# Attention scores of two heads in one pair of PSUM banks, with mask, copy and maximum in one vector operation

## The chip, the cores and the metric

The kernel runs on one core of one Trainium2 chip. The metric is the device time of one execution in microseconds (us), lower is better; several executions are taken and the median is given. Five engines work side by side and meet only through semaphores: TensorE (PE) multiplies matrices, with a queue of its own for loading weights (PEld); VectorE (DVE), ScalarE (ACT) and GpSimd (POOL) work on whole tiles; SyncE (SP) issues most DMA transfers. Matmuls write to PSUM, which has eight banks of 128 partitions by 512 fp32 values.

## The reference

Eight images of 384 channels by 32 x 32 positions, thus 1024 tokens each, pass two layers. All numbers are fp32.

- Layer 0: an RMS norm over channels; a state-space branch (input projection, a causal convolution of four taps, SiLU, then a selective scan with 16 states per channel, once forwards and once backwards); a local branch (3 x 3 depthwise convolution and a sigmoid gate); their sum is added to the input.
- Layer 1, attention: a layer norm over channels, then six heads of size 64 over 1024 tokens, causal. For one head:

```
scores = q @ k^T
scores = where(column <= row, scores, -inf)
attn   = softmax(scores)            # over columns
out    = attn @ v
```

  The heads are joined, projected and added.
- Layer 1, feed-forward: for the first five images only (groups of eight divided by five give one image each): the weights are made binary around their group mean, `h = W1 x + b1` with 1536 rows is scaled by its largest absolute value and clipped, GELU, `W2 h + b2` is quantized in the same way, and the sum is added.

## The kernel before, in words

One image is 3 blocks of 128 channels by 1024 tokens, worked on in halves of 512 columns (`HB`), which is one PSUM bank. The eight banks are shared out by tag: one for `y` (the transposed scan output), two for `da` (the scan's decay factors), one for `av` (weighted values), and two each for `s` and `pt`. The function `bank` (line 101) gives one bank; asked without a tag it alternates between `s` and `pt`. Each bank is a tile of its own, which comes free when its last reader is done.

The work falls into stages that emit steps:

- `before_scan` (norm, projections, convolution, gates, the step size of the scan) takes its banks in turn from the tags that it is given: `s` and `pt` for the first four images, `pt`, `pt`, `av` for those that run later beside feed-forward. `binarize` prepares the feed-forward weights once, at the start; its group means are made in a matmul (line 228) into the bank `av`.
- The scan runs as 768 units of two states each: POOL multiplies `g` (line 588), ACT makes `da` (line 601), DVE scans two states one after the other (line 606), POOL multiplies again (line 612), and PE adds up the result by eight transposing matmuls into `y` (line 620). `g` has six buffers, so POOL can be ahead of PE by that much and no more.
- `attention` projects `op`, `qp`, `vp`, then works through three pairs of heads, two halves of the rows each. A score step (`scores`, lines 767 to 811) takes one block of 128 query rows and up to 512 key columns for the two heads of a pair. The heads lie in the upper and lower 64 rows of PE's array. Each gets its own bank of the tag `s`; the matmuls (line 786) are emitted for head 1 and then head 0, the second with a raised priority so that the two come out together where their banks allow it. In the block on the diagonal a bf16 matmul of an identity with the causal mask (line 797) adds the mask into the last 128 columns. Then, for each head, DVE takes the negated maximum of the bank (line 808) and ACT the exponential with the sum of its row (line 809):

```python
m = nm[:, i, e, kb : kb + 1]
nc.vector.tensor_reduce(m, s, AX.X, ALU.max, negate=True)
nc.scalar.activation(
    pr[:, e, : k1 - k0], s, AF.Exp, bias=m, accum_out=rs[:, i, e, kb : kb + 1]
)
```

  So a score bank is held until ACT has read it. In the step after, `turned` transposes the probabilities on PE (line 861) and ACT copies them (line 863), and `weigh` multiplies them with the values (line 874). There are 288 score steps in all.
- `feed_forward` makes `hp` (line 992), 12 blocks of two halves, and `yp` (line 1037), three blocks of two halves with 12 blocks to add up, each half in a bank of the tag `s`, so that one is filled while ACT empties the other (lines 1000 and 1045).

The order of the work is set in two steps. The program emits slots of the scan in between the steps of the other stages, by costs in microseconds written beside each step and by due times for each image's scan. Then a scheduler that works at build time orders the instructions of each engine by their priority (mostly the order of emission) and hands out the buffers. Each engine runs its own queue strictly in that order. The last image's attention is emitted after everything else.

Of the kernel before, what the change touches and what calls it, by code (L numbers as in the profile page):

```python
# [54 lines left out]
def kernel(  # L55
# [39 lines left out]

    BANKS = {"y": 1, "da": 2, "s": 2, "pt": 2, "av": 1}
    turn = [0]

    def bank(name, tag=None):
        if tag is None:  # L100
            turn[0] += 1
            tag = ("s", "pt")[turn[0] % 2]
        return ps.tile([P, HB], F32, name=name, tag=tag, bufs=BANKS[tag])

    def half(h):
# [51 lines left out]
    make_identity(nc, ident)  # L157
    identb = ctile("identb", [P, P], BF16)
    nc.vector.tensor_copy(identb, ident)
    cmask = mtile("cmask", P)  # L160
    make_causal_mask(nc, cmask, mask_val=MASKED)
    cmaskb = ctile("cmaskb", [P, P], BF16)
    nc.vector.tensor_copy(cmaskb, cmask)
    onesc = ctile("onesc", [P, P])
# [31 lines left out]
    def binarize(src, dst, nk, nout, per, name, emit):  # L196
# [15 lines left out]
        @emit  # L212
        def _():
            st["ones"] = small.tile([P, P], F32, name=f"ones_{name}", tag="bones", bufs=1)
            nc.vector.memset(st["ones"], 1.0 / (gs * nk * P))
            st["mps"] = bank(f"mps_{name}", "av")

        for k in starts:

            @emit  # L220
            def _(k=k, n=min(per, nk - k)):
                v = view(k, n)
                sums = small.tile([P, GROUPS], F32, name=f"sums_{name}_{k}", tag="bsums", bufs=1)
                for g in range(GROUPS):
                    nc.vector.tensor_reduce(
                        sums[:, g : g + 1], v[:, :, g * gs : (g + 1) * gs], AX.XY, ALU.add
                    )
                nc.tensor.matmul(
                    out=st["mps"][:, :GROUPS],
                    lhsT=st["ones"],  # L230
                    rhs=sums,
                    start=(k == 0),
                    stop=(k == starts[-1]),
                )

        @emit
        def _():
            st["mean"] = small.tile([P, GROUPS], F32, name=f"mean_{name}", tag="bmean", bufs=1)
            nc.vector.tensor_copy(st["mean"], st["mps"][:, :GROUPS])

# [17 lines left out]

    def mean_of(c_of, name):

        m = bank(name)
        for c in range(NC):
            nc.tensor.matmul(out=m, lhsT=onesc, rhs=c_of(c), start=(c == 0), stop=(c == NC - 1))
        return m
# [15 lines left out]
    def layernorm(src, name, emit):  # L280

        dst = src
        st = {}
        for h in range(NH):

            @emit.of(6.0)
            def _(h=h):
                mean = mean_of(lambda c: src()[:, c, half(h)], f"mean_{name}_{h}")
                for c in range(NC):
                    nc.vector.tensor_tensor(  # L290
                        dst()[:, c, half(h)], src()[:, c, half(h)], mean, ALU.subtract
                    )
                st[h] = squares(dst(), h, name)

        for h in range(NH):

            @emit.of(6.0)
            def _(h=h):
                var = mean_of(lambda c: st[h][c], f"var_{name}_{h}")
                rstd_of(var, 1)  # L300
                for c in range(NC):
                    nc.vector.tensor_tensor(  # L302
                        dst()[:, c, half(h)], dst()[:, c, half(h)], var, ALU.mult
                    )


    def before_scan(b, tags, emit, later=None, diags=None):
# [5 lines left out]
        def bank_of(name):  # L313
            return bank(name, next(turns))

# [7 lines left out]
        for h in range(NH):  # L323

            @emit
            def _(h=h):
                sqs = squares(st["xn"], h, f"n0_{b}")
                ms = mean_of(lambda c: sqs[c], f"ms_{b}_{h}")
                rstd_of(ms, 0)
# [344 lines left out]
    def attention(b, emit_ffn, emit):  # L674
# [12 lines left out]

        for h in range(NH):
            for m in range(NC):

                @emit
                def _(m=m, h=h):
                    op = bank(f"op_{b}_{m}_{h}")
                    for c in range(NC):
# [19 lines left out]
        for s in range(2):  # L714
            for m in range(NC):
                for h in range(NH):

                    @emit
                    def _(s=s, m=m, h=h):
                        if m == 0 and h == 0:  # L720
                            st["qk"[s]] = btile(f"{'qk'[s]}_{b}")
                        qp = bank(f"qp_{b}_{s}_{m}_{h}")
                        for c in range(NC):
# [9 lines left out]
        for j in range(NT):  # L733

            @emit
            def _(j=j):
                if j == 0:
                    st["v"] = btile(f"v_{b}").rearrange("p c l -> p (c l)").rearrange(
                        "p (j e) -> p j e", e=C
                    )  # L740
                vp = bank(f"vp_{b}_{j}")
                for c in range(NC):
# [24 lines left out]
        def probabilities(c, g, steps):  # L767
# [4 lines left out]
            def scores(i, qi, n, kb, k0, k1):  # L772
# [7 lines left out]
                nm, rs = st["nm", c, g], st["rs", c, g]  # L780
                ss = [bank(f"s_{b}_{c}_{qi}_{kb}_{e}", "s") for e in range(2)]

                order = (1, 0)
                for e in order:
                    with at_once(e == order[1]):
                        mm = nc.tensor.matmul(  # L786
                            out=ss[e][:, : k1 - k0],
                            lhsT=st["q"][rows_of(e), c, chunk(qi)],
                            rhs=st["k"][rows_of(e), c, k0:k1],
                            start=True,  # L790
                            stop=(k1 < n),
                        )
                    if e == order[1]:
                        pin(mm)
                if k1 == n:
                    for e in order:
                        mm = nc.tensor.matmul(  # L797
                            out=ss[e][:, k1 - k0 - P : k1 - k0],
                            lhsT=identb,
                            rhs=cmaskb,  # L800
                            start=False,
                            stop=True,
                        )
                        pin(mm)
                for e in range(2):
                    s = ss[e][:, : k1 - k0]
                    m = nm[:, i, e, kb : kb + 1]
                    nc.vector.tensor_reduce(m, s, AX.X, ALU.max, negate=True)  # L808
                    nc.scalar.activation(  # L809
                        pr[:, e, : k1 - k0], s, AF.Exp, bias=m, accum_out=rs[:, i, e, kb : kb + 1]  # L810
                    )
# [108 lines left out]
        for m in range(NC):  # L920
            for h in range(NH):

                @emit
                def _(m=m, h=h):
                    if h == 0:
# [4 lines left out]
                        st["to"] = to  # L930
                    op = bank(f"ap_{b}_{m}_{h}")
                    for c in range(NC):
# [21 lines left out]
    def quant_scale(mx, name):  # L954

        col = small.tile([P, 1], F32, name=f"col_{name}", tag="col")
        nc.vector.tensor_reduce(col, mx, AX.X, ALU.max)
        row = bank(f"row_{name}", "s")
        nc.tensor.transpose(row[:, :P], col.to_broadcast([P, P]), ident)
# [7 lines left out]
    def feed_forward(b, t, emit):  # L967
# [9 lines left out]
        for m in range(NF):  # L977
            for h in range(NH):

                @emit.of(3.1)  # L980
                def _(m=m, h=h):
                    if m % NC == 0 and h == 0:
                        st["h", m // NC] = btile(f"h{m // NC}_{b}")
                    if m % 2 == 0 and h == 0:
# [4 lines left out]
                        )  # L989
                    hp = bank(f"hp_{b}_{m}_{h}", "s")  # L990
                    for c in range(NC):
# [6 lines left out]
                        )  # L998
                    hm = st["h", m // NC][:, m % NC, :]
                    nc.scalar.activation(hm[:, half(h)], hp, AF.Identity, bias=b1t[:, m : m + 1])  # L1000
                    if h == NH - 1:
                        nc.vector.tensor_reduce(
                            st["mxh"][:, m : m + 1], hm, AX.X, ALU.max, apply_absolute_value=True
                        )
# [16 lines left out]
        for m in range(NC):  # L1021
            for h in range(NH):

                @emit.of(10.7)
                def _(m=m, h=h):
                    if m == 0 and h == 0:
                        st["y"] = btile(f"yf_{b}")
                    if h == 0:
                        for k in range(0, NF, 6):
# [4 lines left out]
                            st["w2", k // 6] = w  # L1034
                    yp = bank(f"yp_{b}_{m}_{h}", "s")
                    for k in range(NF):
# [6 lines left out]
                        )  # L1043
                    ym = st["y"][:, m, :]
                    nc.scalar.activation(
                        ym[:, half(h)], yp, AF.Identity, bias=vec[:, m, V_B2 : V_B2 + 1]
                    )
                    if h == NH - 1:
                        nc.vector.tensor_reduce(
                            st["mxy"][:, m : m + 1], ym, AX.X, ALU.max, apply_absolute_value=True  # L1050
# [6 lines left out]
        for m in range(NC):  # L1057

            @emit
            def _(m=m):  # L1060
                to = mtile(f"t3_{b}_{m}")
                load(to, spilled[b, "t2", m])
                for h in range(NH):
                    ym = bank(f"yq_{b}_{m}_{h}", "s")
                    nc.vector.tensor_scalar(
                        ym, st["y"][:, m, half(h)], st["s2"], QCLIP, ALU.mult, ALU.min
                    )
                    th = to[:, half(h)]
                    nc.vector.scalar_tensor_tensor(th, ym, -QCLIP, th, ALU.max, ALU.add)
                nc.sync.dma_start(out=out[b, chunk(m), :], in_=to)  # L1070
# [66 lines left out]
    begin = Steps()  # L1137
    before_scan(ORDER[0], ("s", "pt"), begin, beside)
    run(begin)
    beside += steps_of(before_scan, ORDER[1], ("s", "pt"), diags=diags)  # L1140
    beside += steps_of(binarize, w1, w1s, NC, FF, 2, "w1")
    beside += steps_of(binarize, w2, w2s, NF, C, 8, "w2")
    for b in ORDER[2 : 1 + ahead]:
        beside += steps_of(before_scan, b, ("s", "pt"), diags=diags)
    run(first, beside)
# [76 lines left out]
```

## Time and profile before

Three executions took 5177.72 to 5191.12 us, with a median of 5189.24. The profiled one took 5184.05 us and its span is 5182.2 us.

| engine | busy us | share of the span |
|---|---|---|
| PE | 4203.1 | 81% |
| PEld | 2254.6 | 44% |
| DVE | 3562.3 | 69% |
| ACT | 2701.1 | 52% |
| POOL | 3688.1 | 71% |

A page of the profile gives for each group of instructions the line, the engine, the operation, the tiles written and read, the shapes and the count; then the busy time and the mean of one in ns; then the time that the engine stood idle just ahead of such instructions, and what it waited for. An fp32 matmul counts as two instructions (two passes). Matmuls are pipelined, so the mean duration of one is longer than the time from one to the next. The table of waits sums idle time by who waited and for whom. Idle time of an engine that sets no pace costs nothing.

### The profile page before, as it was taken

The numbers are of one execution on the slowest core, as the hardware profiler recorded it, in microseconds if no ns is written. First come the engines' busy times: TensorE is split into PE (matmuls) and PEld (weight loads), VectorE is DVE, ScalarE is ACT, GpSimd is POOL, SyncE is SP. The second block draws the span as 40 slices with busy tenths as digits, with TensorE's granted clock in tenths as the row PEclk, the third lists the DMA queues.
The fourth block names the chain that finished last, engine by engine and source line by source line (L and its number), as shares of the span: only waits on it lengthen the run. The fifth ranks groups of instructions, "written<-read, shape, count | busy, mean of one in ns | idle before, by whom it ended". The sixth has DMA issues, their size and how long they took to land. (4 is left out here: it accounts for less than half of the span.)

```text
span 5182.2 us, 51037 instructions
## 1 busy us (share of the span) xinstructions
PE 4203.1 (81%) x16842; PEld 2254.6 (44%) x16842; DVE 3562.3 (69%) x4206; ACT 2701.1 (52%) x4891; POOL 3688.1 (71%) x1944
## 2 busy tenths in 40 slices
PE   3687787888878788888887888878889888888798
PEld 1243443444434444444543444434445444444444
DVE  6887887667886667876687856778666665565522
ACT  4565564555645556545556445564454454453334
POOL 0578687877679776787777788677878977787600
PEclk7788797889889899898998888988988889989888
DMA  6554545324463234543343533336333234224200
GB/s 228 197 184 152 200 167 190 111 80 156 152 216 114 88 103 146 198 143 112 109 153 121 201 126 103 118 125 221 122 103 126 88 106 166 87 70 150 82 33 25
DMA packets 365009, 696.38 MB, mean 134 GB/s; under 512 B 30104, under 2 KB 88904, under 8 KB 364744
## 3 DMA queue, kind: packets, MB, share of 16 engines
q1 hardware_dynamic: 355232, 676.97, 38.8%
q10 hardware_dynamic: 9512, 16.15, 0.9%
q8 instruction: 133, 2.18, 0.2%
q14 instruction: 132, 1.08, 0.1%
HBM read 527.33 MB, written 165.68 MB: 134 GB/s over the span
## 5 line engine op out<-in xcount | busy, mean ns | idle before, releaser
L588 POOL TENSOR_TENSOR g<-ud,bc 128x1024 f32<-128x1024 f32 x768 | 1836.3, 2391 | 737.0 <-PE y L620 586.5
L612 POOL TENSOR_TENSOR g<-g,bc 128x1024 f32<-128x1024 f32 x768 | 1818.8, 2368 | 229.8 <-DVE g L606 177.2
L601 ACT ACTIVATE da<-dl,amat 128x512 f32<-128x512 f32 x1536 | 1059.6, 692 | 1648.4 <-DVE g L606 1606.5
L606 DVE TENSOR_TENSOR_SCAN g<-da,carry,g 128x512 f32<-128x512 f32 x768 | 955.9, 1271 | 461.6 <-POOL g L588 430.2
L606 DVE TENSOR_TENSOR_SCAN g<-da,g 128x512 f32<-128x512 f32 x768 | 904.2, 1209 | 514.4 <-POOL g L588 496.9
L620 PE MATMUL y<-ident,g 128*128 128x128 f32 x6144 | 948.4, 301 | 272.7 <-POOL g L612 204.3
L620 PEld LDWEIGHTS y<-ident,g 128*128 128x128 f32 x6144 | 787.7, 156 | 663.0 <-POOL g L612 325.3
L786 PE MATMUL s<-k,q 64*128 64x512 f32 (+3 forms) x1152 | 443.6, 616 | 182.3 <-ACT pr L809 172.3
L808 DVE TENSOR_REDUCE nm<-s 128x1 f32<-128x512 f32 (+3 forms) x576 | 293.4, 543 | 231.0 <-PE s L797 154.9
L861 PE MATMUL pt<-ident,pr 128*128 128x128 f32 x1728 | 334.9, 315 | 80.0 <-ACT ptn L863 49.0
L809 ACT ACTIVATE pr<-s,nm 128x512 f32<-128x512 f32 (+3 forms) x576 | 327.8, 573 | 123.5 <-DVE nm L808 122.7
L992 PE MATMUL hp<-t,w 128*128 128x512 f32 x720 | 339.1, 616 | 25.8 <-DMA w<-w1s 15.1
L341 PE MATMUL in<-xn,win 128*128 128x512 f32 x576 | 295.2, 655 | 49.7 <-DVE xc L463 16.6
L1037 PE MATMUL yp<-h,w 128*128 128x512 f32 x720 | 327.5, 612 | 9.0 <-DMA w<-w2s 8.9
L861 PEld LDWEIGHTS pt<-ident,pr 128*128 128x128 f32 x1728 | 221.5, 159 | 238.7 <-ACT ptn L863 118.5
L863 ACT COPY ptn<-pt 128x512 f32<-128x512 f32 (+3 forms) x576 | 264.0, 480 | 101.8 <-PE pt L861 100.1
L874 PE MATMUL av<-ptn,v 128*64 128x512 f32 (+3 forms) x1152 | 287.9, 575 | 35.8 <-DVE o L888 21.0
L786 PEld LDWEIGHTS s<-k,q 64*128 64x128 f32 x1152 | 164.3, 212 | 323.6 <-ACT pr L809 254.8
L725 PE MATMUL qp<-t,wqk 128*128 128x512 f32 x576 | 263.0, 606 | 18.4 <-DVE t L302 13.0
L400 DVE SCALAR_TENSOR_TENSOR loc<-xn,vec,loc 128x496 f32<-128x496 f32 (+3 forms) x384 | 260.4, 721 | 23.6 <-ACT loc L389 22.2
L611 POOL COPY carry<-g 128x2 f32<-128x2 f32 x384 | 83.4, 217 | 248.0 <-DVE g L606 240.3
L1037 PEld LDWEIGHTS yp<-h,w 128*128 128x128 f32 x720 | 139.8, 198 | 176.3 <-issue 165.4
(157 smaller groups left out, 4817.3 us busy)
## 6 DMA issues: line engine op xcount, KB each, us to landing
bc<-rows SPq DMA_DIRECT2D x512, 512.0 KB, 4.1
dl<-sdl SPq DMA_DIRECT2D x160, 256.0 KB, 2.9
ud<-sud SPq DMA_DIRECT2D x160, 256.0 KB, 2.7
t<-st SPq DMA_DIRECT2D x63, 512.0 KB, 5.3
su<-u SPq DMA_DIRECT2D x48, 512.0 KB, 3.7
du<-su SPq DMA_DIRECT2D x96, 256.0 KB, 4.3
sdl<-du SPq DMA_DIRECT2D x96, 256.0 KB, 2.9
sud<-du SPq DMA_DIRECT2D x96, 256.0 KB, 2.7
```

What stands on the lines that cost most here:

```text
L341: nc.tensor.matmul(out=mp, lhsT=st["win", c][:, k, i, :], rhs=st["xn"][:, k, half(h)], start=(k == 0), stop=(k == NC - 1),)
L588: pin(nc.gpsimd.tensor_tensor(g, ud, sst["bc", 0, u.b, u.part, u.n], ALU.mult))
L601: nc.scalar.activation(da, sst["dl", u.b, u.c, u.part], AF.Exp, scale=amat[:, u.c, n : n + 1])
L606: nc.vector.tensor_tensor_scan(gi[:, ::step], da[:, ::step], gi[:, ::step], first, ALU.mult, ALU.add)
L612: pin(nc.gpsimd.tensor_tensor(g, g, sst["bc", 1, u.b, u.part, u.n], ALU.mult))
L620: nc.tensor.matmul(out=y[:, j, :], lhsT=g[:, i, chunk(j)], rhs=ident, is_transpose=True, start=(u.opens and i == 0 and j == 0), stop=(u.cl ...
L786: mm = nc.tensor.matmul(out=ss[e][:, : k1 - k0], lhsT=st["q"][rows_of(e), c, chunk(qi)], rhs=st["k"][rows_of(e), c, k0:k1], start=True, st ...
L808: nc.vector.tensor_reduce(m, s, AX.X, ALU.max, negate=True)
L809: nc.scalar.activation(pr[:, e, : k1 - k0], s, AF.Exp, bias=m, accum_out=rs[:, i, e, kb : kb + 1])
L861: nc.tensor.transpose(pt[:, chunk(i)], pr[:, e, chunk(j % QT)], ident)
L992: nc.tensor.matmul(out=hp, lhsT=st["w1"][:, c, chunk(m % 2)], rhs=st["xn"][:, c, half(h)], start=(c == 0), stop=(c == NC - 1),)
L1037: nc.tensor.matmul(out=yp, lhsT=st["w2", k // 6][:, k % 6, :], rhs=st["h", k // NC][:, k % NC, half(h)], start=(k == 0), stop=(k == NF - 1),)
```

## The change

The two banks of the tag `s` become one tile of two neighbouring banks, a pair. The scores of two heads fill one pair, always together. The causal mask is no longer added on PE: one vector operation reads a head's bank, adds the mask, multiplies by -1, writes the result to SBUF and takes the minimum, which is the negated maximum that the exponential needs as its bias. Blocks off the diagonal take a zero column of the mask, repeated. The exponential then works in place in SBUF, with a scale of -1. This operation, `tensor_tensor_reduce` with an output for the minimum, is built as two vector instructions, the second one writing the minimum.

The other stages that used `s` take pairs as well: `op`, `qp`, `vp`, `ap` and the layer norms' mean and variance alternate between a pair and two banks of `pt`; `hp`, `yp` and the quantization of the output use the pair as 1024 columns, emptied by one operation; `before_scan` of the first images rotates through `s` (half of a pair), `pt`, `av`, `pt`; the weights' group means move from `av` to a pair. The purpose is to take work from PE, to free the score banks earlier, and to empty banks in fewer operations.

The diff, cut to its core:

```diff
-    BANKS = {"y": 1, "da": 2, "s": 2, "pt": 2, "av": 1}
+    BANKS = {"y": 1, "da": 2, "s": 1, "pt": 2, "av": 1}
...
+    def pair(name):
+        return ps.tile([P, 2, HB], F32, name=name, tag="s", bufs=BANKS["s"])
+
+    def two_banks(name):
+        turn[0] += 1
+        if turn[0] % 2:
+            p = pair(name)
+            return [p[:, i, :] for i in range(2)]
+        return [bank(f"{name}_{i}") for i in range(2)]
...
+    cmask = ctile("cmask", [P, HB], BF16)
+    nc.vector.memset(cmask, 0.0)
+    masked = mtile("masked", P)
+    make_causal_mask(nc, masked, mask_val=MASKED)
+    nc.vector.tensor_copy(cmask[:, HB - P :], masked)
...
-            st["mps"] = bank(f"mps_{name}", "av")
+            st["mps"] = pair(f"mps_{name}")[:, 0, :]
...
-                        qp = bank(f"qp_{b}_{s}_{m}_{h}")
+                        if h == 0:
+                            st["qp"] = two_banks(f"qp_{b}_{s}_{m}")
+                        qp = st["qp"][h]
...
-                ss = [bank(f"s_{b}_{c}_{qi}_{kb}_{e}", "s") for e in range(2)]
-
-                order = (1, 0)
-                for e in order:
-                    with at_once(e == order[1]):
+                ss = pair(f"s_{b}_{c}_{qi}_{kb}")[:, :, : k1 - k0]
+                for e in range(2):
+                    with at_once(e == 1):
                         mm = nc.tensor.matmul(
-                            out=ss[e][:, : k1 - k0],
+                            out=ss[:, e, :],
                             lhsT=st["q"][rows_of(e), c, chunk(qi)],
                             rhs=st["k"][rows_of(e), c, k0:k1],
                             start=True,
-                            stop=(k1 < n),
-                        )
-                    if e == order[1]:
+                            stop=True,
+                        )
+                    if e == 1:
                         pin(mm)
-                if k1 == n:
-                    for e in order:
-                        mm = nc.tensor.matmul(
-                            out=ss[e][:, k1 - k0 - P : k1 - k0],
-                            lhsT=identb,
-                            rhs=cmaskb,
-                            start=False,
-                            stop=True,
-                        )
-                        pin(mm)
+
+                w = k1 - k0
+                mask = cmask[:, HB - w :] if k1 == n else cmask[:, :1].to_broadcast([P, w])
                 for e in range(2):
-                    s = ss[e][:, : k1 - k0]
-                    m = nm[:, i, e, kb : kb + 1]
-                    nc.vector.tensor_reduce(m, s, AX.X, ALU.max, negate=True)
+                    x, m = pr[:, e, :w], nm[:, i, e, kb : kb + 1]
+                    nc.vector.tensor_tensor_reduce(
+                        out=x,
+                        in0=ss[:, e, :],
+                        in1=mask,
+                        scale=-1.0,
+                        scalar=-MASKED,
+                        op0=ALU.add,
+                        op1=ALU.min,
+                        accum_out=m,
+                    )
                     nc.scalar.activation(
-                        pr[:, e, : k1 - k0], s, AF.Exp, bias=m, accum_out=rs[:, i, e, kb : kb + 1]
+                        x, x, AF.Exp, bias=m, scale=-1.0, accum_out=rs[:, i, e, kb : kb + 1]
                     )
...
-                    hp = bank(f"hp_{b}_{m}_{h}", "s")
+                    if h == 0:
+                        st["hp"] = pair(f"hp_{b}_{m}")
+                    hp = st["hp"][:, h, :]
...
-                    hm = st["h", m // NC][:, m % NC, :]
-                    nc.scalar.activation(hm[:, half(h)], hp, AF.Identity, bias=b1t[:, m : m + 1])
                     if h == NH - 1:
+                        hm = st["h", m // NC][:, m % NC, :]
+                        nc.scalar.activation(
+                            hm,
+                            st["hp"].rearrange("p h l -> p (h l)"),
+                            AF.Identity,
+                            bias=b1t[:, m : m + 1],
+                        )
...
-                    yp = bank(f"yp_{b}_{m}_{h}", "s")
+                        st["yp"] = pair(f"yp_{b}_{m}")
+                    yp = st["yp"][:, h, :]
...
-    before_scan(ORDER[0], ("s", "pt"), begin, beside)
+    before_scan(ORDER[0], ("s", "pt", "av", "pt"), begin, beside)
```

## The prediction

> **What bounds the kernel now.** I read the engines' totals first, then the windows by stage, then the table of waits, then the groups.
>
> ```profile
> PE 4203.1 (81%) x16842; PEld 2254.6 (44%) x16842; DVE 3562.3 (69%) x4206; ACT 2701.1 (52%) x4891; POOL 3688.1 (71%) x1944
> ```
>
> No engine is full, but TensorE (PE) is the fullest. The windows say where (columns: window, its length, then busy us and instruction count of PE, PEld, DVE, ACT, POOL, then clock and DMA): one of attention beside scans, one of the stage before the scans beside feed-forward, and the end, where the last image's attention runs without scans.
>
> ```profile
> 3770.00:3900.00 130.00, 108.34 (x573) 62.11 (x573) 76.01 (x98) 69.66 (x165) 99.23 (x63) 0.83 0.29 96
> 2860.00:2990.00 130.00, 102.70 (x307) 52.35 (x306) 107.05 (x122) 57.25 (x93) 94.08 (x56) 0.84 0.55 189
> 4923.00:5182.00 259.00, 237.10 (x912) 110.15 (x912) 64.93 (x129) 97.24 (x258) 0.00 (x0) 0.87 0.08 29
> ```
>
> Attention loads PE (83%, at the end 92%) and leaves VectorE (DVE) 42% free. The other stage loads DVE (82%). The waits (engine and line, releaser: us in total, times, longest):
>
> ```profile
> ACT da L601 <- DVE g L606: 1606.5, 1104, 11.1
> POOL g L588 <- PE y L620: 586.5, 211, 11.3
> PEld s L786 <- ACT pr L809: 254.8, 273, 6.3
> PE s L786 <- ACT pr L809: 172.3, 141, 6.0
> ```
>
> The second row is the key one: GpSimd (POOL), which feeds the scan, stands 587 us because PE has not yet transposed the scan's output and so not freed a `g` buffer. PE works through one queue, in which transposes stand between attention's matmuls; what delays a score matmul delays the scan. The last row is such a delay: the score matmul finds its PSUM bank still held by the exp of the step before. In the attention window above, POOL makes 21 pairs of multiplications in 130 us, 6.2 us each, where two multiplications of 2.36 us take 4.7: POOL can follow a faster PE. So I treat PE time in attention as time of the kernel.
>
> The groups I price from (busy us, mean ns | idle before):
>
> ```profile
> L786 PE MATMUL s<-k,q 64*128 64x512 f32 (+3 forms) x1152 | 443.6, 616 | 182.3 <-ACT pr L809 172.3 <-DVE v L750 4.9 <-ACT v L750 4.2
> L797 PE MATMUL s<-cmaskb,identb 128*128 128x128 bf16 x384 | 61.9, 250 | 0.0
> L808 DVE TENSOR_REDUCE nm<-s 128x1 f32<-128x512 f32 (+3 forms) x576 | 293.4, 543 | 231.0 <-PE s L797 154.9 <-PE s L786 75.3
> L809 ACT ACTIVATE pr<-s,nm 128x512 f32<-128x512 f32 (+3 forms) x576 | 327.8, 573 | 123.5 <-DVE nm L808 122.7
> L809 ACT ACTIVATION_READ_ACCUMULATOR pr<-s,nm 128x1 f32 x576 | 113.3, 197 | 0.0
> L290 DVE TENSOR_TENSOR t<-t,mean_na 128x512 f32<-128x512 f32 x48 | 30.1, 676 | 12.8 <-PE mean_na L263 7.9 <-DMA st<-t 3.0 <-PE y L620 1.8
> L703 DVE SCALAR_TENSOR_TENSOR t<-op,rssm,t 128x512 f32<-128x512 f32 x48 | 34.4, 734 | 21.2 <-PE op L695 21.1
> L1000 ACT ACTIVATE h<-hp,b1t 128x512 f32<-128x512 f32 x120 | 80.3, 675 | 38.6 <-PE hp L992 38.4
> L434 ACT ACTIVATE u<-u 128x1024 f32<-128x1024 f32 x48 | 50.2, 1056 | 0.6
> ```
>
> [...]
>
> **The change part by part.**
>
> *Masks leave PE.* 384 bf16 matmuls go, 61.9 us of PE. Their weight loads stand idle another 97 us on the load queue, mostly beside other matmuls. Between 45 and 90; I take 62.
>
> *The two heads' score matmuls stay together.* They lie on different 64-row halves of the array. In the last attention four 512-wide passes of such a pair take 1.13 us, where twelve full-height passes of L992 take 5.15, 0.43 each: the heads run at the same time, and apart they would need four times 0.43, 1.72. In the built order of before, other work stands between the heads in 77 of the 288 score steps, since each head waits for its own bank; with one pair tile, the order of after has 288 of 288 together. A split costs 0.6 us at 512 and, at the mean width of 384, 0.45: 77 x 0.45 = 35 us. Low 20, high 50.
>
> *The bank comes free earlier.* Before, from the scores' end: two maxima and the last exp with its accumulator read, 0.54 + 0.54 + 0.57 + 0.20 = 1.85 us at the mean width, and that exp queues behind `da` exponentials that wait for scans (the 1606 us row). Now the DVE operation writes negated masked scores to SBUF, and exp works there: the pair is free after two DVE operations and their reads. An operation at 384 is 676 - 133 = 543 ns by L290 [...] or 734 - 133 = 601 by L703: I take 0.57. The read lies between 0.06 (the smallest memset of the trace, 59 ns) and 0.20 (ScalarE's): I take 0.13. Together 2 x 0.70 = 1.4 us, 0.45 less, and one queue fewer. The head that used to be free first now waits for both, a loss inside the same wait. Of the 172 us on PE I let 95 go; between 40 and 150.
>
> *DVE pays.* 576 x (0.57 + 0.13 - 0.51) = 109 us, with 0.51 = 293.4/576; between 60 and 160. DVE goes from 69% to 71%, and in the attention window from 76 to about 83 of 130. What queues behind are scans, and POOL behind those (it waits 177 us for scans today). I let a quarter through: 27 us; between 0 and 60.
>
> *Exp from SBUF.* Same width, another source, ScalarE at 54% in the attention window: nothing, hidden behind PE. `ptn` copies wait no longer than before.
>
> *Feed-forward on one pair.* `hp` and `yp` had two banks in turn; now 75 pairs share one tile, evicted by one activation of 1024 elements (1.06 by L434, against 2 x 0.675: ScalarE saves 22 us, hidden). The new wait: the next pair's first matmul stands behind that activation, and behind it in PE's queue stand the scan's transposes. In the built order some 2 us of other PE work lies between one `hp` pair and the next (1.2 to 4.3, of transposes and input projections), against 1.06 plus the hand-over. Mostly hidden; a late ScalarE gives perhaps 0.3 us each: 22 us, between 0 and 100 (75 x 1.3).
>
> *Other users of the pair* (`op`, `qp`, `vp`, `ap`, layer norm) keep four banks in rotation, only freed two at a time: 10 us. In the first stage four banks rotate as before, but the weights' mean takes the pair where it had a bank unused at that time, so the binarization moves from the first 100 vector instructions to the 350th. DVE is at 65% in the first 130 us and 87% in the next two windows, so work moved out of the idle start costs: 15 us, between 0 and 40. Halved quantization (`yq`) and dropped memsets: some 5 us of DVE, hidden.
>
> Sum: 62 + 35 + 95 - 27 - 22 - 10 - 15 = 118 us of gain. 5189 - 118 = 5071; I say 5070.
>
> **The rivals.**
>
> *Slower: DVE becomes the bound.* If the new operation runs at half rate, it takes about 1.0 us at the mean width, the pair's chain grows to 2.3 us, longer than before, and DVE gets 576 x (1.0 + 0.13 - 0.51) = 357 us. With half of that on the path (scans sit in that queue), and the waits not shrinking but growing by 40, against 97 from masks and pairing: 5189 + 178 + 40 - 97 + 47 = 5357; with full rate but every feed-forward wait exposed (100), DVE's 60 and the start's 40: 5189 - 62 - 35 - 40 + 100 + 60 + 40 + 10 = 5262. For it: DVE is nearly full outside attention. Against: [...]attention is where DVE has room.
>
> *No change: the waits move.* PE's score wait turns from ACT into DVE at the same length, as scans of 1.2 us stand in between, and the additions eat the masks: 5189 - 62 - 35 + 27 + 22 + 10 + 15 = 5166, with somewhat more wait 5185. For it: POOL, DVE and PE feed each other in a ring, and PE still waits 204 us for POOL. Against: the last attention has no scans, waits 15 us at L786 and spends 7.9 us on masks; it must gain.
>
> *Much faster.* All score waits but a few vanish (150), masks are worth 90, pairing 50, no new stall: 5189 - 290 + 20 = about 4920.
>
> **How the numbers follow.** Forecast, within about 60 us: 0.56. Much faster: 0.12. Waits move: 0.16, half of it still a little faster than 0.3%. Slower: 0.16. So faster 0.56 + 0.12 + 0.07 = 0.75, same 0.08, slower 0.17. The range runs from 4960 to 5215: above it is most of the slower case, below it half of the much faster one.
>
> **What would show it.** Right: the score matmuls wait for the new vector line, under 110 us on PE; no mask line; busy time of the score matmuls falls below 420 us with fewer split pairs; POOL waits for PE under 500 us; the last attention, from its first `op` matmul, takes 235 to 245 us instead of 259; the new vector operation takes 0.68 to 0.74 at 512 and its read 0.06 to 0.20. Wrong: the operation over 0.9 us at 512; scans that wait behind it so that POOL's wait for scans passes 300 us; `hp` matmuls that wait over 50 us for their activation; a first `y` transpose or a last scan that comes later than today. An instruction order that the planner changes by chance could also shift the stages by more than the terms I priced.

## The result, and the profile after

The changed kernel takes 5243.63 us (median of four executions, 5241.31 to 5251.63), the kernel before 5187.74 in the same comparison. The ratio is 1.0114, with a 95% interval of 1.0096 to 1.0131: it is slower by about 56 us, where a gain of 118 was forecast.

The totals of the changed kernel's page (busy us, share, instructions):

```profile
PE 4073.2 (78%) x16458; PEld 2177.5 (41%) x16458; DVE 3606.6 (69%) x4755; ACT 2701.9 (51%) x4812; POOL 3703.7 (71%) x1944
```

PE has 130 us less to do than before (4203.1) and the span is 67.6 us longer (5249.8 against 5182.2). So PE stands idle 198 us more. The granted clock of the whole run does not explain that: it is 0.872 to 0.876 in the four executions, and 0.870 to 0.877 in those of the kernel before that were taken beside the experiments. The waits of the changed kernel that answer to those shown of before, with the bank waits of the projections and of feed-forward added:

```profile
ACT da L612 <- DVE g L617: 1642.5, 1110, 10.7
POOL g L599 <- PE y L631: 724.8, 216, 16.0
PEld s L801 <- DVE nm L815: 254.8, 138, 6.2
PE s L801 <- DVE nm L815: 206.9, 112, 6.0
PE hp L1012 <- ACT h L1021: 50.7, 21, 8.4
PE op L708 <- DVE t L716: 31.9, 14, 6.2
PE vp L760 <- ACT v L767: 15.9, 11, 2.1
PE ap L951 <- DVE t L959: 14.4, 7, 3.7
PE qp L740 <- DVE k L747: 14.4, 7, 2.1
```

POOL waits 138 us longer for PE's transposes (586.5 before): the ring of POOL, scan and PE has become slower. The last five rows are new or longer. In the kernel before, PE waited 3.2 us at `op` for the reader of an earlier `op`, and `vp` and `ap` had no idle time at all. The groups of the changed kernel (busy, mean ns of one | idle before):

```profile
L801 PE MATMUL s<-k,q 64*128 64x512 f32 (+3 forms) x1152 | 310.0, 620 | 215.6 <-DVE nm L815 206.9 <-ACT v L767 6.3 <-DVE v L767 2.0
L815 DVE CUSTOM_DVE_ANT_0 pr<-s,cmask 128x512 f32<-128x512 f32 (+3 forms) x576 | 293.4, 546 | 148.5 <-PE s L801 115.1 <-PE pt L877 33.0
L815 DVE DVE_READ_ACCUMULATOR2_ANT nm<- 128x1 f32 x576 | 47.5, 82 | 0.0
L1021 ACT ACTIVATE h<-hp,b1t 128x1024 f32<-128x1024 f32 x60 | 66.2, 1103 | 42.0 <-PE hp L1012 41.8
```

At 512 columns the new operation, with mask, scaling and output, takes as long as the plain maximum of before:

```profile
L808 DVE TENSOR_REDUCE nm<-s 128x1 f32<-128x512 f32 x288 | 185.9, 676 | 102.7 <-PE s L786 75.3 <-PE s L797 27.2
L815 DVE CUSTOM_DVE_ANT_0 pr<-s,cmask 128x512 f32<-128x512 f32 x288 | 184.8, 679 | 37.6 <-PE s L801 37.4
```

The first row of L815 is the new vector operation; its accumulator read, 82 ns, is a row of its own. The mask matmuls are gone. The score matmuls are busy for 310 us instead of 444, but wait longer.

The stages tell where the time went. Going by when the same scan starts in both traces, the changed kernel lags 27 us at the 97th scan, 53 at the 577th, 79 at the 1057th and 103 at the 1489th of 1536; then the last attention takes back 38. The end, from the last scan on (columns as in the windows of before; first the kernel before, then the changed one):

```profile
4899.00:5182.00 283.00, 251.32 (x985) 119.14 (x983) 77.02 (x150) 99.10 (x261) 5.49 (x3) 0.87 0.10 37
```

```profile
5005.00:5250.00 245.00, 213.10 (x936) 100.94 (x934) 77.66 (x217) 99.42 (x260) 5.40 (x3) 0.95 0.11 43
```

There the score stage, from its first to its last vector operation, falls from 146 to 104 us. So the change gains where no scans run; beside the scans something eats more than it brings. The 38 us need not all be the banks' doing, however: the granted clock (third number from the end) is 0.95 in this stretch against 0.87. As an estimate from these shares, 283 x 0.13 = 37 us of full clock were withheld before and 245 x 0.05 = 12 now, so up to 25 of the 38 us may be clock. Whether the shorter waits raised the clock is not shown.

### The profile page after: what moved, and what is told of

It is laid out like the page before. It is cut to its first block, busy times and chain, and to the rows that moved or that the text cites. A ratio compares the mean times of both kernels' runs of the same rounds, so it can differ in the third digit from the quotient of the medians.

```text
span 5249.8 us, 50688 instructions
## 1 busy us (share of the span) xinstructions
PE 4073.2 (78%) x16458; PEld 2177.5 (41%) x16458; DVE 3606.6 (69%) x4755; ACT 2701.9 (51%) x4812; POOL 3703.7 (71%) x1944
## 5 line engine op out<-in xcount | busy, mean ns | idle before, releaser
L599 POOL TENSOR_TENSOR g<-ud,bc 128x1024 f32<-128x1024 f32 x768 | 1842.5, 2399 | 868.1 <-PE y L631 724.8
L623 POOL TENSOR_TENSOR g<-g,bc 128x1024 f32<-128x1024 f32 x768 | 1826.7, 2379 | 262.4 <-DVE g L617 173.3
L801 PE MATMUL s<-k,q 64*128 64x512 f32 (+3 forms) x1152 | 310.0, 620 | 215.6 <-DVE nm L815 206.9
L877 PE MATMUL pt<-ident,pr 128*128 128x128 f32 x1728 | 323.4, 308 | 113.1 <-ACT ptn L879 74.5
L815 DVE CUSTOM_DVE_ANT_0 pr<-s,cmask 128x512 f32<-128x512 f32 (+3 forms) x576 | 293.4, 546 | 148.5 <-PE s L801 115.1
L825 ACT ACTIVATE pr<-pr,nm 128x512 f32<-128x512 f32 (+3 forms) x576 | 347.9, 606 | 77.4 <-DVE nm L815 76.4
L1012 PE MATMUL hp<-t,w 128*128 128x512 f32 x720 | 344.2, 624 | 51.8 <-ACT h L1021 50.7
L1063 PE MATMUL yp<-h,w 128*128 128x512 f32 x720 | 324.6, 608 | 14.5 <-DMA w<-w2s 10.2
L877 PEld LDWEIGHTS pt<-ident,pr 128*128 128x128 f32 x1728 | 208.2, 153 | 307.4 <-ACT ptn L879 151.8
L740 PE MATMUL qp<-t,wqk 128*128 128x512 f32 x576 | 285.6, 646 | 43.0 <-DVE t L312 23.8
L890 PE MATMUL av<-ptn,v 128*64 128x512 f32 (+3 forms) x1152 | 275.1, 562 | 21.4 <-DVE o L904 12.5
L1012 PEld LDWEIGHTS hp<-t,w 128*128 128x128 f32 x720 | 136.7, 198 | 218.8 <-issue 146.2
L801 PEld LDWEIGHTS s<-k,q 64*128 64x128 f32 x1152 | 99.3, 211 | 306.2 <-DVE nm L815 254.8
```

What stands on the lines that cost most here:

```text
L599: pin(nc.gpsimd.tensor_tensor(g, ud, sst["bc", 0, u.b, u.part, u.n], ALU.mult))
L623: pin(nc.gpsimd.tensor_tensor(g, g, sst["bc", 1, u.b, u.part, u.n], ALU.mult))
L740: nc.tensor.matmul(out=qp, lhsT=st["wqk"][:, c, o : o + P], rhs=st["xn"][:, c, half(h)], start=(c == 0), stop=(c == NC - 1),)
L801: mm = nc.tensor.matmul(out=ss[:, e, :], lhsT=st["q"][rows_of(e), c, chunk(qi)], rhs=st["k"][rows_of(e), c, k0:k1], start=True, stop=True,)
L825: nc.scalar.activation(x, x, AF.Exp, bias=m, scale=-1.0, accum_out=rs[:, i, e, kb : kb + 1])
L877: nc.tensor.transpose(pt[:, chunk(i)], pr[:, e, chunk(j % QT)], ident)
```

## Experiments

All results are given as the ratio to the kernel before in the same comparison. Its median was 5185.7 to 5190.8 us in these comparisons, so a difference of a few us between two runs means nothing.

Two theories stood at the start: the hand-over of banks in pairs costs (P), or the vector operation costs, as banks now wait in VectorE's queue (D).

**The operation alone.** The kernel before, with separate score banks, and only the vector operation taken over. To make room in SBUF for the wider mask, the group means use the common matrix of ones, as in the changed kernel.

```diff
-                    nc.vector.tensor_reduce(m, s, AX.X, ALU.max, negate=True)
...
+                    nc.vector.tensor_tensor_reduce(
+                        out=x,
+                        in0=ss[e][:, :w],
+                        in1=mask,
+                        scale=-1.0,
+                        scalar=-MASKED,
+                        op0=ALU.add,
+                        op1=ALU.min,
+                        accum_out=m,
+                    )
```

> The kernel before with the new vector operation alone: each head keeps its own score bank, op, qp, vp, ap, hp, yp and the layer norms keep their single banks. If the loss comes from handing banks over in pairs (theory P), the operation alone gains: 5060 to 5130 us, and the waits of PE at op, qp, vp, ap and hp stay at the sum of before, 65 us. If the operation itself is the cost (theory D: the banks now wait in VectorE's queue behind scans, and scans behind the operation), it is no faster than before: 5180 to 5260 us.

Measured: 5047.58 us, ratio 0.9725 (0.9709 to 0.9741). The operation alone gains some 141 us, and theory D falls. Its score group and its operation:

```profile
L785 PE MATMUL s<-k,q 64*128 64x512 f32 (+3 forms) x1152 | 405.4, 609 | 124.2 <-DVE nm L798 113.3 <-DVE v L749 4.9 <-ACT v L749 4.2
L798 DVE CUSTOM_DVE_ANT_0 pr<-s,cmask 128x512 f32<-128x512 f32 (+3 forms) x576 | 301.2, 546 | 212.0 <-PE s L785 185.3 <-PE pt L860 26.0
```

Busy and idle time of the score matmuls come to 405.4 + 124.2 = 530 us, against 310.0 + 215.6 = 526 with the pair, and in the last attention the score stage takes 98 us against 104 (the granted clock of the whole profiled run is 0.881, against 0.872). So at the scores themselves the pair brings almost nothing that the operation doesn't bring with separate banks.

**The pairs alone.** The changed kernel with the old mask matmuls, the old reduction and the exponential from PSUM.

> The changed kernel with masks on PE, maximum by the old reduction and exponential from PSUM: only the pairs are left. Theory P: slower than before by the added bank waits, 121 us at op, qp, vp, ap and hp, and by more score waits, since the pair needs both exponentials: 5270 to 5350 us. Theory D: about as before, 5180 to 5210 us.

Measured: 5861.52 us, ratio 1.1297 (1.128 to 1.1314), far beyond what theory P expected. A pair is now held until both exponentials are done. The idle time of PE that ends with an exponential goes from 172 us, all at the scores, to 314: 141.9 at the scores and 171.6 at the transposes of the probabilities. The built order shows a second cause. In all 288 score steps the maximum of the second head carries a wait for ScalarE's exponential of the first head, though that reads the other bank of the pair; in the kernel before, none of the 288 does. So VectorE stands still, with scans behind in its queue, and POOL's wait for PE more than doubles (586.5 before):

```profile
DVE nm L825 <- ACT pr L826: 126.2, 143, 1.9
POOL g L600 <- PE y L632: 1253.1, 128, 129.1
```

No run shows how the loss divides between the two. With the new operation VectorE alone reads the pair, and in the changed kernel none of its second heads carries a wait. So the two parts of the change depend on each other. The operation is worth 141 us with separate banks and 618 with pairs (5861.5 to 5243.6). The pairs cost 196 us with it (5047.6 to 5243.6) and about 673 without.

**Single banks for the projections.** The changed kernel, but `op`, `qp`, `vp`, `ap`, mean and variance take banks one by one.

```diff
-    def two_banks(name):
+    def single(name):
         turn[0] += 1
-        if turn[0] % 2:
-            p = pair(name)
-            return [p[:, i, :] for i in range(2)]
-        return [bank(f"{name}_{i}") for i in range(2)]
+        tag = ("s", "pt", "av", "pt")[turn[0] % 4]
+        return pair(name)[:, 0, :] if tag == "s" else bank(name, tag)
...
-                        if h == 0:
-                            st["qp"] = two_banks(f"qp_{b}_{s}_{m}")
-                        qp = st["qp"][h]
+                        qp = single(f"qp_{b}_{s}_{m}_{h}")
```

> The changed kernel, but op, qp, vp, ap and the layer norms rotate through four banks that come free one by one (half of the pair, pt, av, pt). Theory P: PE's waits at op, qp, vp and ap fall from 134 us to about 40, and the time by 60 to 95 us, to 5150 to 5185. Theory D: within 15 us of the changed kernel, 5230 to 5260.

Measured: 5117.85 us, ratio 0.9864 (0.9849 to 0.9878): 126 us less than the changed kernel, and more than theory P expected. PE's idle time at `op`, `qp`, `ap` and `vp` is 35 us instead of 134. First the changed kernel, then this one, where `ap` and `vp` have none:

```profile
L708 PE MATMUL op<-gy,wout 128*128 128x512 f32 x288 | 155.6, 694 | 54.6 <-DVE t L716 31.9 <-DVE du L538 13.5 <-DMA gy<-sgy 7.4
L740 PE MATMUL qp<-t,wqk 128*128 128x512 f32 x576 | 285.6, 646 | 43.0 <-DVE t L312 23.8 <-DVE k L747 14.4 <-ACT q L747 4.0
L951 PE MATMUL ap<-o,wproj 128*128 128x512 f32 x288 | 137.1, 624 | 14.4 <-DVE t L959 14.4
L760 PE MATMUL vp<-wv,t 128*128 128x384 f32 x384 | 135.6, 499 | 22.1 <-ACT v L767 15.9 <-DVE v L767 6.2
```

```profile
L700 PE MATMUL op<-gy,wout 128*128 128x512 f32 x288 | 147.1, 661 | 15.4 <-DVE du L532 6.2 <-DVE t L1080 4.8 <-DVE t L708 3.5
L730 PE MATMUL qp<-t,wqk 128*128 128x512 f32 x576 | 264.2, 609 | 20.0 <-DVE t L306 12.2 <-issue 5.6 <-DVE q L737 2.0
POOL g L593 <- PE y L625: 600.1, 201, 12.5
```

More was gained than these 99 us, and POOL's wait for PE, the last row, falls by 125 us, from 724.8: a late PE holds up POOL too. This is the largest single loss of the change.

**Emptied by halves.** The changed kernel, `hp` and `yp` emptied by two activations of 512.

```diff
+                    hm = st["h", m // NC][:, m % NC, :]
+                    nc.scalar.activation(hm[:, half(h)], hp, AF.Identity, bias=b1t[:, m : m + 1])
                     if h == NH - 1:
-                        hm = st["h", m // NC][:, m % NC, :]
-                        nc.scalar.activation(
-                            hm,
-                            st["hp"].rearrange("p h l -> p (h l)"),
-                            AF.Identity,
-                            bias=b1t[:, m : m + 1],
-                        )
```

> The changed kernel, but each half of hp and yp is emptied by its own 512-wide activation, as before; the pair stays one tile. Theory P, if the length of the last eviction (1.10 us against 0.67) makes the hp wait: PE's wait at hp falls from 52 us to about 30, time 5215 to 5235. If the wait is ScalarE's queue, or the missing second buffer as such, no change: 5235 to 5260. Theory D: no change.

Measured: 5318.91 us, ratio 1.0253 (1.0238 to 1.0268): slower by 75 us than the changed kernel, which no theory expected. The idle time at feed-forward rises from 51.8 us at `hp` and 14.5 at `yp` to:

```profile
L1012 PE MATMUL hp<-t,w 128*128 128x512 f32 x720 | 358.7, 636 | 68.4 <-ACT h L1020 68.0
L1058 PE MATMUL yp<-h,w 128*128 128x512 f32 x720 | 347.6, 642 | 39.7 <-ACT yf L1066 27.3 <-DMA w<-w2s 10.4 <-DVE h L1039 1.9
```

The built programs show why. In this kernel the first matmul of the second half carries a wait for ScalarE's reading of the first half in 59 of 60 `hp` tiles and 15 of 15 `yp`; in the changed kernel in none. Where a reader of the first half stands between the two halves, the build makes the second half's matmuls wait for it, though they write another bank: it guards the tile as a whole. The same holds for the projections of the changed kernel, in 62 of their 64 pair tiles. A piece of PE's built order (x2 stands for two matmuls alike):

```
Matmult qp_7_1_0 128x512 [waits Activation]
Matmult qp_7_1_0 128x512 x2
Matmult qp_7_1_1_0 128x512 [waits Activation]
Matmult qp_7_1_0 128x512 [waits Activation]
Matmult qp_7_1_0 128x512 x2
```

The tile `qp_7_1_0` is a pair: its first half waits for the slot, and its fourth matmul, the first of the second half, waits again. One matmul of the next block, into the single bank `qp_7_1_1_0`, is put in between. In the trace of the changed kernel one sees the wait at the end of the last image's projections, with no scan to disturb (time, duration, engine; PE, then ACT; in brackets the idle time before):

```profile
5107.61 2.20 PE L760 MATMUL vp<-wv,t 128*128 128x384 f32 x6 [0.57 <-ACT v L767]
```

```profile
5107.08 0.48 ACT L767 COPY v<-vp 128x384 f32<-128x384 f32 x1 [1.46 <-PE vp L760]
```

The copy ends at 5107.56, and the matmuls of the second half start 0.05 us later, after 0.57 us of idle PE.

**Both halves before the emptying.** This gave a third theory, L (lock), against W, that only the shorter rotation of banks costs. The changed kernel keeps its pairs, but in the projections both halves are multiplied before either is read:

```diff
-                        nc.any.tensor_copy(st["qk"[s]][:, m, half(h)], qp)
+                        if h < NH - 1:
+                            return
+                        for i in range(NH):
+                            nc.any.tensor_copy(st["qk"[s]][:, m, half(i)], st["qp"][i])
```

> The changed kernel with its pairs, but in op, qp, vp, ap and the layer norms both halves are emptied after the second half's matmuls, not the first half in between. Theory L (lock: in one tile the second half's matmuls are made to wait for the reader of the first half): PE's waits at op, qp, vp and ap fall from 134 us to under 60, the time to 5110 to 5165 us. Theory W (window: a pair comes free only as a whole, so the rotation of banks is shorter): no gain, as the first half is emptied even later: 5240 to 5290 us.

Measured: 5160.46 us, ratio 0.9937 (0.9922 to 0.9951). With the same pairs in the same banks, 83 us of the 126 come back, and the kernel is now faster than before. In the built order none of the 64 pair tiles has a wait for a reader in the middle; idle time at the four projections is 59 us (31.9 + 27.2 + 0 + 0). Theory L holds for two thirds. The remaining 43 us fit theory W, that a pair comes free as a whole, but no run isolates that; the run with single banks also takes the bank `av` into the rotation.

**Feed-forward on single banks.** The run with single projections, and `hp` and `yp` in single banks too, each emptied by itself.

> The run with single banks for the projections, and hp and yp in single banks as well (half of the pair, pt, av, pt in turn, each half emptied by its own activation). If the rest of the loss against the operation alone, 70 us, lies in feed-forward on one pair, its wait at hp falls from 58 us to about 25 and the time to 5075 to 5095 us. Against it: the projections for later images use pt and av at the same time, so the wait may only move there: then 5110 to 5140.

Measured: 5214.98 us, ratio 1.005 (1.0031 to 1.0068): 97 us slower than with the pair, and beyond both expectations. The idle time at `hp` does fall, to 37.8 us, mostly for weights; but the projections of later images, which run beside it on `pt` and `av`, now wait:

```profile
L346 PE MATMUL in<-xn,win 128*128 128x512 f32 x576 | 282.9, 638 | 107.9 <-ACT up L353 59.7 <-DVE xn L337 15.4 <-ACT u L384 14.5
L492 PE MATMUL xp<-u,wx 128*64 128x512 f32 x192 | 92.9, 750 | 67.9 <-ACT u L439 25.9 <-ACT yf L1049 14.2 <-ACT u L384 11.8
```

In the run with the pair for feed-forward these idle times are 71.3 and 42.4, and POOL's wait for PE is 600 us against 718 here. So the wait moves and grows; of the two ways tried with these eight banks, the pair is the better one for feed-forward.

**The place of the binarization.** First the group means in a `da` bank instead of the pair:

```diff
-            st["mps"] = pair(f"mps_{name}")[:, 0, :]
+            st["mps"] = bank(f"mps_{name}", "da")
```

> The run with single banks for the projections, and the weights' group means in a bank of the tag da, which is unused until the first scan. If the pair's slot pushed the binarization into the full stretch before 500 us, the 49th unit of two scans comes at about 475 us again instead of 508, and the time falls by 20 to 35 us, to 5083 to 5098. If that stretch has slack later, no change: 5110 to 5125.

Measured: 5115.65 us, ratio 0.9851 (0.9836 to 0.9866), no change beyond a few us. The binarization had not moved: in the trace all but its first five vector operations still run at 376 to 449 us (26 to 123 in the kernel before). So the edit tells nothing about its place. Together with feed-forward on single banks:

> Both of the last two edits: only the scores, the quantization and one transpose still use pairs. If the parts add up, 5045 to 5075 us, level with the operation alone (5048), and pairs for the scores then cost nothing. If the pair of the scores is itself a cost, it stays above 5085.

Measured: 5210.23 us, ratio 1.0042 (1.0027 to 1.0057), as with the feed-forward edit without it and far above what was expected. A second edit, from the run with single projections, puts the group means back on `av` and takes `av` from the first images' rotation:

```diff
-            st["mps"] = pair(f"mps_{name}")[:, 0, :]
+            st["mps"] = bank(f"mps_{name}", "av")
...
-    before_scan(ORDER[0], ("s", "pt", "av", "pt"), begin, beside)
+    before_scan(ORDER[0], ("s", "pt", "pt"), begin, beside)
```

> The run with single banks for the projections, but the group means in the bank av, as before, and the first images' projections on half of the pair and two pt. In the built order the binarization is back among the first vector instructions; the last edit with the tag da had not moved it (it ran at 376 to 449 us, with 26 to 123 in the kernel before). If its place causes the lag of the first stage, the 49th unit of two scans comes at 475 to 485 us instead of 508, and the time falls by 15 to 30 us, to 5088 to 5103. If the rotation of three banks costs as much, no change: 5105 to 5125.

Measured: 5088.85 us, ratio 0.9813 (0.9794 to 0.9832), 29 us less than the run with single projections. The binarization is done by 119 us, and the 97th scan comes at 479 us, as in the kernel before (477), instead of 508. Three banks in rotation are enough for the first stage.

**The heads' order**, in the kernel with the operation alone: `order = (0, 1)` for `(1, 0)`.

> The operation alone, with the heads' score matmuls in the order 0, 1 (as VectorE takes them) instead of 1, 0. If the first matmul of a step often waits for the head that VectorE empties last, PE's wait at the scores falls from 113 us to about 80 and the time to 5015 to 5035 us. If the two heads lie together anyway (258 of 288), no difference beyond the noise: 5040 to 5055.

Measured: 5050.62 us, ratio 0.974 (0.9718 to 0.9761): no difference beyond a few us. The operation alone remains the fastest version found, 2.7% below the kernel before and 3.7% below the changed one (5047.58/5243.63 = 0.963).

## Why the prediction was wrong

*The step that failed* is the one on other users of the pair: "keep four banks in rotation, only freed two at a time: 10 us". I counted the banks and took the halves as free of each other. They are not: the build guards a tile as a whole, so the second half's matmuls wait for the first half's reader. It cost 126 us instead of 10, of which 83 are shown to be this lock; of the 174 us between forecast and result this term makes 116. The built order was in my working, but I read in it only which tiles follow each other, not the waits that they carry.

*Masks*: right, 61.9 us of PE gone.

*Pairing and earlier banks*: the sum was about right, its split wrong. Busy and idle time of scores and masks together go from 443.6 + 182.3 + 61.9 = 688 to 310.0 + 215.6 = 526 us, a gain of 162 against 62 + 35 + 95 = 192. But busy time fell by 134 us instead of 35, and the wait grew by 33 instead of falling by 95. And nearly the whole gain is the operation's: with separate banks it is 158 us (688 to 530). Two heads that merely follow each other in the order still wait each for its own bank: on average 1.22 us pass between the starts of the first and the last of a step's four passes beside scans before, 1.12 with the operation alone and 0.53 in the changed kernel, where both heads wait once and then run together. What is saved between the heads is lost in waiting ahead of them. With scans about, 2.35 us pass from the scores' end to the first vector operation (1.40 before), and for 1.55 us of these VectorE is in scans (1.02 before); in the last attention it is 0.29. So beside scans the pair is held for 4.47 us from its first matmul, against 5.28 of before to the last exponential; in the last attention for 2.27 against 4.13. I had let ScalarE's queue fall out of the chain and put no wait for VectorE's queue in its place; the rival in which the waits only move had named this one.

*DVE pays*: 47 us more at this line (293.4 + 47.5 - 293.4) instead of 109. The price was too high, as was my 0.13 for the accumulator read (82 ns): the operation costs as much as the reduction (679 ns against 676 at 512 elements). The 133 ns that I took off for 128 elements fit: at 384 the reduction takes 542 ns and the operation 544. That the operation would keep the pace of L290 and L703 was my assumption, which no row of before showed, and so was the half rate of the slower rival: its 1.0 us at the mean width of 384 did not come. The trace of before shows no such pace even for two fp32 sources in SBUF: L526 is a scalar_tensor_tensor of 512 elements with two such sources and no accumulator, and its shortest and median times are 666 and 693 ns (the long ones are under *POOL*):

```profile
L526 DVE SCALAR_TENSOR_TENSOR dp<-ew x96: 666/693/2854, 113.5 to 3616.2; 128x512 f32<-128x512 f32 x96
```

*Exp from SBUF*: 606 ns against 573 on average (713 against 680 at 512), 20 us more in all. No run shows whether it was hidden, as I said.

*Feed-forward on one pair*: 22 us expected; idle time at `hp` and `yp` rose by 31 us (34.8 to 66.3). *First stage*: 15 expected, 29 measured by undoing.

*POOL*: my sum has no term for it, and it kept its length (2399 and 2379 ns, 2391 and 2368 before). The new operation, too, takes the same time beside POOL as without it: at 512 elements 692 ns at most in the 216 cases that overlap a POOL instruction, 693 in the other 72. It reads one operand from PSUM. L526, which reads both from SBUF, took 701 ns at most in the 44 cases of before that overlap no POOL instruction, and 1939 at the median, 2854 at most, in the other 52.

The first half of the sum, 62 + 35 + 95 - 27 = 165, is near the 141 us that the operation brought by itself. That is in part luck: the 35 were priced for one pair, and this run has none; its heads still come out together more often, with other work between them in 30 of the 288 steps instead of 77. The second half, 22 + 10 + 15 = 47, was 196. Of these 126 (projections) and 29 (binarization) are shown by undoing; 41 us are left between 5088.85 and 5047.58. PE's idle time at `hp` differs by 33 us there (58.7 against 25.4), so feed-forward's single pair is a likely place, but no run isolates it from the scores' pair, since single banks for feed-forward disturbed the projections beside it.

Of my signs of being right, two failed: PE's wait for the new vector line is 206.9 us, not under 110, and POOL's wait for PE 724.8, not under 500. One sign of being wrong came, if barely: `hp` waits 50.7 us for its activation, over 50. The last attention, from its first `op` matmul, takes 223 us, less than the 235 to 245 that I named, and 209 with the operation alone. The rival that ended slower named other causes (a slow vector operation, full exposure of feed-forward); it was right in direction alone.

## What to carry to other kernels

Before joining two buffers into one tile, read in the built order which instructions carry waits, not only which follow each other: a scheduler that guards tiles as a whole turns "read half 0, write half 1" into a stall, even in separate banks, and two engines that read a half each into a queue. If both halves must share a tile, write both and then empty both. And try the parts of a compound change apart: here the operation was worth 2.7% by itself, and the pair, which brought almost nothing at the scores, hid it.

## What the runs showed of the hardware

Adding a bf16 mask, scaling and writing 512 fp32 results to SBUF took VectorE 679 ns in the changed kernel, the plain maximum of 512 values from PSUM 676 ns in the kernel before; only the accumulator read of 82 ns is new. Emptying a pair by one activation of 1024 took 1103 ns in the changed kernel, against 2 x 675 for halves in the kernel before. The pairs of score matmuls on the two 64-row halves of the array, started together, take 1.13 us for four passes of 512 (the median and the shortest of 144 steps of the changed kernel; the median of before is 1.68), where full-height passes take 0.43 each (the median from one start to the next at `hp`, without the longer gaps, in both kernels). A scalar_tensor_tensor with two fp32 sources of 512 elements in SBUF has a median of 693 ns in the kernel before, and of 686 in the 44 cases without a POOL instruction beside it.
